# Layer norm from running sums, masks for two heads at a time, and another order for the first feed-forward products

## The chip, the core and the metric

The kernel runs on one core of one Trainium2 chip. A core has five engines that run side by side, each through its own list of instructions in order: TensorE (PE in the profile; its weight loads are PEld) multiplies matrices into PSUM, VectorE (DVE) and ScalarE (ACT) work on rows of up to 128 partitions, GpSimd (POOL) does small things, and SyncE (SP) issues transfers. They wait for each other by semaphores. The metric is the device time of one execution in microseconds. Before the change it is 3044.09 us, the median of three runs (3042.1 to 3045.04).

## What is computed

64 graphs of 256 nodes with 256 features go through two layers. All is float32.

```python
# layer 0, per graph
h = gat(gat(x, adj, W1, a1), adj, W2, a2)      # softmax over masked, leaky sums of two vectors, times rows
h = ln(x + h)
h = ln(h + relu(h @ w_ff1 + b) @ w_ff2 + b)    # 256 -> 1024 -> 256
# layer 1, per graph: 8 heads of 32, values chosen by adj
attn = softmax(q @ k.T / sqrt(32))
out = sum over r of (attn * (adj == r)) @ v_r
x = ln(h + out @ Wo + bo)
x = ln(x + gelu(x @ W1 + b1) @ W2 + b2)
```

`ln` subtracts the mean of a row of 256, divides by the root of its variance plus 1e-5, multiplies by g and adds beta. It is done four times for each graph.

## The kernel before

Two graphs make a pair, and a pair takes the whole way: the two graph layers (`gat_layers`, L528 to L557), a feed-forward (stage 0), the attention, a feed-forward (stage 2). Rows lie as 128 partitions by 256 features, four such blocks a pair. The first feed-forward product (L681) needs the rows transposed; each feed-forward does it with seven products of quarter blocks instead of eight (class `Blocks`, steps p1 to p7 for two slabs a and b). Between these stand copies on ScalarE (L687), additions on VectorE (L392) and activations (L693): product 6 can start when the copy of product 1 is there, 7 after the copy of 6, 4 after that of 7. The second product (L712) sums over the 1024 hidden columns.

The order of all instructions is written by a planner, not by hand. Python generators, one for each pair, yield the steps of TensorE with the events and PSUM banks they need; `put` hands a piece of work to one of the other engines with an estimated duration, a rank and events. `run` (L213) keeps a clock for each engine, takes whichever engine can go on first, and emits its next piece; each engine then runs its pieces in that order. Four pairs are under way at a time, besides a short generator at the start. Only one pair may be in the graph layers, one in the attention and one in a feed-forward of either stage (`alone`). Of the steps that could go, TensorE takes those outside a feed-forward first, then those of the oldest pair; so feed-forwards fill the gaps of the rest.

Around the change:
- `add_rows` (L570) adds a product from PSUM to the rows of a graph. `layernorm` then takes statistics on VectorE (L582 to L585), the power -0.5 on GpSimd (L588, L589), the normalising on ScalarE (L593), g and beta on VectorE (L598).
- `transposed` turns 32 by 32 blocks on VectorE (L618), stores to memory (L623) and gathers from it with four transfers (L629); SP issues them.
- In the graph layers a row of 1024 numbers is stored (L478) and spread to all partitions (L482) before VectorE weighs with it (L499, L501) and ScalarE scales by the inverse of the sums (L509).
- In the attention a quarter is one graph and four heads. `scores` makes its products (L796, arrays of 32 rows), ScalarE the exponentials (L803), VectorE the masked copy (L807) and the sum of two halves (L811); `products` multiplies with the values (L825) and sums columns (L828, arrays of 32 columns). VectorE inverts the sums (L837), multiplies (L838), and ScalarE reads the largest values for a check of ranges (L835). `into_rows` (L847) applies Wo.

Tiles for these are handed out in turn from pools: eight of a, m and h each with one head.

A second kernel for inputs outside the ranges is in the program too; it is not run here.

## Time and profile before

| | us |
|---|---|
| median of three runs | 3044.09 |
| profiled execution, first to last instruction | 3047.2 |
| TensorE busy | 2996.3 |
| VectorE busy | 2556.8 |
| ScalarE busy | 1752.5 |
| GpSimd busy | 252.6 |

The profiled execution has its own time, 3.1 us above the median. Its page gives the busy time of each engine, then groups of instructions by line with their number, their busy time, the mean duration of one and the idle time of the engine before them. In the waits, "A <- B: 9.1, 18, 1.4" says that A waited 9.1 us in total for B, 18 times, at most 1.4. In the timeline a line has the start and the length in us, engine, line, operation, out<-in and the number of instructions merged; in brackets stands the idle time before and what ended it. A float32 product shows as two records. The granted clock of TensorE was 0.995 over the span.

### The profile page before, as it was taken

The page shows a single profiled execution, that of the slowest core. Times are in us where ns is not written, and L with a number is a line of the kernel's source. Part 1 is how long each engine was busy: PE and PEld are TensorE (multiplying, and loading weights), DVE is VectorE, ACT ScalarE, POOL GpSimd, SP SyncE. Part 2 cuts the span into 40 slices and gives each one's busy share as a digit, 9 for nine tenths or more (in the row PEclk, how much of TensorE's full clock was granted, in tenths as well). Part 3 has the DMA queues.
Part 4 walks back from the last instruction along what each step waited for, and adds up shares of the span by engine and source line. Part 5 has one row for each costly group of instructions (what it writes and reads, how often), then busy time and mean ns, then how long its engine had stood idle before and what let it go on. Part 6 is the DMA issues. An engine that isn't in the chain of part 4 may idle for free.

```text
span 3047.2 us, 52870 instructions
## 1 busy us (share of the span) xinstructions
PE 2996.3 (98%) x19146; PEld 2452.5 (80%) x19146; DVE 2556.8 (84%) x5993; ACT 1752.5 (58%) x4096; POOL 252.6 (8%) x518
## 2 busy tenths in 40 slices
PE   7999999999999999999999999999999999999998
PEld 6887788878888888888888888888888888788876
DVE  5888988788988888888889888889888898888875
ACT  4556666556556556555565565565555655555654
POOL 0100010001100001100001000011000011000100
PEclk8999999999999999999999999999999999999999
DMA  5211041212212222112222112221122221122100
GB/s 186 74 47 61 32 127 54 70 56 84 70 40 66 77 84 77 53 53 70 84 84 77 39 60 77 84 77 62 50 68 79 84 77 52 52 71 70 49 1 22
DMA packets 211147, 205.76 MB, mean 68 GB/s; under 512 B 22336, under 2 KB 170432, under 8 KB 210880
## 3 DMA queue, kind: packets, MB, share of 16 engines
q1 hardware_dynamic: 210464, 202.06, 20.6%
q8 instruction: 153, 2.51, 0.4%
q14 instruction: 114, 0.93, 0.1%
q10 hardware_dynamic: 416, 0.26, 0.0%
HBM read 137.51 MB, written 64.73 MB: 66 GB/s over the span
## 4 chain that ended last, share of the span: by engine, by line
PE 63%; DVE 25%; DMA 6%; ACT 2%; SPq 1%; issue 1%; POOL 0%; DVEq 0%; ACTq 0%; POOLq 0%
PE ps L712 21%; PE ps L681 15%; PE ps L825 5%; DVE x L598 4%; PE ps L759 4%; PE ps L754 4%; PE ps L544 3%; DVE h L837 3%; PE ps L796 3%; DMA home<-yb 3%; DVE st L582 2%; DVE m L807 2%; PE ps L557 2%; DMA rows<-row 2%; DVE ff L392 2%; PE ps L847 2%
## 5 line engine op out<-in xcount | busy, mean ns | idle before, releaser
L712 PE MATMUL ps<-w_L_gnn_w_ff,ff 128*128 128x256 f32 x2048 | 470.9, 381 | 0.0
L712 PE MATMUL ps<-w_L_gnn_W,ff 128*128 128x256 f32 x2048 | 456.1, 380 | 1.8 <-ACT ff L693 1.8
L593 ACT ACTIVATE x<-x,less,rstd 128x256 f32<-128x256 f32 x512 | 279.2, 596 | 294.8 <-POOL less L589 294.7
L712 PEld LDWEIGHTS ps<-w_L_gnn_w_ff,ff 128*128 128x128 f32 x2048 | 386.6, 190 | 61.5 <-issue 9.8
L712 PEld LDWEIGHTS ps<-w_L_gnn_W,ff 128*128 128x128 f32 x2048 | 388.2, 190 | 57.6 <-ACT ff L693 2.6
L588 POOL TENSOR_TENSOR rstd<-rstd,mhalf 128x2 f32<-128x2 f32 x256 | 198.3, 775 | 2765.7 <-DVE less L585 2638.0
L807 DVE TENSOR_TENSOR m<-a,adj 128x512 f32<-128x512 f32 x512 | 350.1, 684 | 57.9 <-ACT a L803 57.8
L803 ACT ACTIVATE a<-ps 128x512 f32<-128x512 f32 x512 | 268.0, 604 | 222.6 <-PE ps L796 222.5
L681 PE MATMUL ps<-yT,w_L_gnn_W1p 128*128 128x256 f32 x1280 | 315.2, 382 | 4.7 <-ACT ff L687 2.4
L392 DVE TENSOR_TENSOR ff<-ps,ff 128x512 f32<-128x512 f32 x384 | 262.7, 685 | 66.4 <-PE ps L681 58.3
L681 PE MATMUL ps<-yT,w_L_gnn_w_ff1p 128*128 128x256 f32 x1280 | 308.8, 382 | 6.8 <-ACT ff L687 5.9
L681 PEld LDWEIGHTS ps<-yT,w_L_gnn_w_ff1p 128*128 128x128 f32 x1280 | 240.6, 190 | 50.8 <-ACT ff L687 18.8
L687 ACT ACTIVATE ff<-ps 128x512 f32<-128x512 f32 x384 | 223.9, 590 | 98.4 <-PE ps L681 97.6
L681 PEld LDWEIGHTS ps<-yT,w_L_gnn_W1p 128*128 128x128 f32 x1280 | 240.2, 190 | 48.2 <-ACT ps L835 8.5
L837 DVE RECIPROCAL h<-ps 128x256 f32<-128x256 f32 x128 | 223.4, 1746 | 21.3 <-PE ps L828 20.9
L509 ACT ACTIVATE xw<-xw,rs 128x258 f32<-128x258 f32 (+1 forms) x256 | 115.9, 502 | 200.7 <-DVE rs L504 200.6
L693 ACT ACTIVATE ff<-ff,c_L_gnn_b_ff 128x256 f32<-128x256 f32 x384 | 171.6, 504 | 97.4 <-DVE ff L392 97.0
L693 ACT ACTIVATE ff<-ff,c_L_gnn_b 128x256 f32<-128x256 f32 x384 | 173.3, 501 | 85.0 <-DVE ff L392 83.8
L811 DVE TENSOR_TENSOR h<-a 128x256 f32<-128x256 f32 x512 | 213.9, 418 | 0.0
L582 DVE BATCH_NORM_STATS2 st<-x 128x6 f32<-128x256 f32 x512 | 206.0, 402 | 0.9
L570 DVE TENSOR_TENSOR x<-ps,x 128x512 f32<-128x512 f32 x256 | 170.2, 682 | 16.4 <-PE ps L712 9.3
L769 ACT ACTIVATE qk<-ps,bqk 128x256 f32<-128x256 f32 x256 | 106.6, 468 | 112.2 <-PE ps L754 111.9
(128 smaller groups left out, 5008.1 us busy)
## 6 DMA issues: line engine op xcount, KB each, us to landing
home<-yb SPq DMA_DIRECT2D x182, 256.0 KB, 2.0
yT<-home SPq DMA_DIRECT2D x728, 64.0 KB, 2.0
rows<-row SPq DMA_DIRECT2D x60, 512.0 KB, 4.0
input<-in_xT SPq DMA_DIRECT2D x32, 512.0 KB, 5.1
x<-in_x SPq DMA_DIRECT2D x32, 512.0 KB, 3.8
out<-x SPq DMA_DIRECT2D x32, 512.0 KB, 5.1
input<-in_adjT SPq DMA_DIRECT2D x30, 512.0 KB, 4.5
v<-in_adjT SPq DMA_DIRECT2D x2, 512.0 KB, 7.3
```

The lines of the kernel that those rows point to most:

```text
L392: nc.vector.tensor_tensor(self.target(c, h), self.bank[bank], self.target(c, h), ALU.add)
L582: nc.vector.bn_stats(st[:, j, :], rows[j])
L588: nc.gpsimd.tensor_tensor(rstd, rstd, mhalf[:, :2], ALU.pow)
L593: nc.scalar.activation(rows[j], rows[j], AF.Identity, bias=less[:, j:j + 1], scale=rstd[:, j:j + 1])
L681: nc.tensor.matmul(to, lhsT=w1[:, a, (t + slab) * P:(t + slab + 1) * P], rhs=b, **flags)
L687: return put("scalar", 0.5, lambda: nc.scalar.activation(target(c, h), blocks.bank["x"], AF.Copy), event, rank=-1)
L693: evacuated[h][m] = put("scalar", 0.4, lambda m=m, to=to, source=source: nc.scalar.activation(to, source, func, bias=b1[:, m:m + 1]), even ...
L712: nc.tensor.matmul(p2[:, j * D:(j + 1) * D], lhsT=f[m][:, (2 * j + b) * P:(2 * j + b + 1) * P], rhs=w2[:, m, :], start=m == 0, stop=m == N ...
L803: nc.scalar.activation(a[n][o], ps[o], AF.Exp)
L807: nc.vector.tensor_tensor(m[n][o], a[n][o], adj, ALU.mult)
L811: nc.vector.tensor_tensor(h[n][o], a[n][o][:, :N], a[n][o][:, N:], ALU.add)
L837: there = put("vector", 1.68, lambda: nc.vector.reciprocal(s, po[:, N:]), there, rank=0)
```

## The change

- Layer norm: the row addition is done row block by row block with a running sum, which times -1/256 is minus the mean (`less`). ScalarE takes the squares of the centred rows with a running sum into a tile that nobody reads (`unread`). VectorE centres and multiplies by g in one operation, GpSimd makes the power -0.5, VectorE multiplies by it and adds beta in one operation. In a feed-forward both graphs' layer norms are planned after its last product.
- Masks and halves are made for two heads at a time; a, m and h are four tiles of two heads.
- The inverse of the sums: VectorE transposes 32 by 32 blocks, copies out eight columns, inverts these and transposes back. The check reads the eight columns.
- `products` are planned for each quarter alone, with the later scores between them, instead of two quarters together.
- `put_each` plans what was one piece with two parts as two pieces.
- TensorE's choice: first feed-forward products come first, the graph layers and attention next, second products last. The number of pairs under way rises by two steps of one at the start; one of them goes when the generator at the start has ended, so that five pairs are under way.
- Planned durations and ranks follow, and the tiles of the feed-forward are cut by quarters of the result (`f[c][h]`). A form of the second product with seven products (`by_seven`) is added, but `SEVEN` is empty, so it is never called.

Lines that only rename or set planned durations, and `by_seven` with its helpers (`means`, `last_weights`, `last_sums`), are left out:

```diff
+SEVEN = ()
...
+    unread = const.tile([P, N], F32, name="unread")
...
+        piece["first"] = behind.piece["first"] if behind else piece
+        piece["event"].piece = piece
...
+    def put_each(engine, us, emits, *events, rank=1, frees=(), needs=None, function=None):
+        before = None
+        for emit in emits[:-1]:
+            before = put(engine, us, emit, *events, rank=rank, lag=0.0, needs=needs, function=function, behind=before)
+            events, needs = [before], None
+        return put(engine, us, emits[-1], *events, rank=rank, frees=frees, function=function, behind=before)
...
         going, ways = [[besides, *next(besides)]], iter(ways)
+        together += 1
+        def degree(g):
+            if g[0] in filling:
+                return 2
+            return 0 if "ff" in (g[2] or ()) or alone.get("ff") is g[0] else 1
         together += 1
...
-                g = going[min(sure, key=lambda n: (going[n][0] is besides, "ff" in (going[n][2] or ()) or alone.get("ff") is going[n][0], n))
+                g = going[min(sure, key=lambda n: (going[n][0] is besides, degree(going[n]), n))
...
-                piece = waiting[engine].pop(min(able, key=lambda n: (waiting[engine][n]["rank"], waiting[engine][n]["ready"])))
+                piece = waiting[engine].pop(min(able, key=lambda n: (waiting[engine][n]["rank"], waiting[engine][n]["first"]["ready"])))
...
-        rows = y[:, of_graph(b), :].rearrange("p k d -> p (k d)")
-        return put("vector", 0.6, lambda: nc.vector.tensor_tensor(rows, p, rows, ALU.add), *events, frees=["bank"])
-    def layernorm(r, gb, b, *events):
+        of = {}
+        def add(j):
+            if j == 0:
+                of["less"] = small.tile([P, 2], F32, name="less", bufs=8)
+            row = y[:, 2 * b + j, :]
+            nc.vector.scalar_tensor_tensor(row, p[:, j * D:(j + 1) * D], 1.0, row, op0=ALU.mult, op1=ALU.add,
+                                           accum_out=of["less"][:, j:j + 1])
+            if j == 1:
+                nc.vector.tensor_scalar(of["less"], of["less"], -1.0 / D, None, ALU.mult)
+        return of, put_each("vector", 0.44, [lambda j=j: add(j) for j in range(2)], *events, frees=["bank"])
...
+    def layernorm(r, gb, b, added, *events):
         g, beta, _ = gb
-        st = mv = rstd = less = None
+        of, there = added
+        squares = rstd = None
         rows = [r[:, 2 * b + j, :] for j in range(2)]
-        def statistics():
-            nonlocal st, mv, rstd, less
-            st, mv = small.tile([P, 2, 6], F32, name="st"), small.tile([P, 2, 2], F32, name="mv")
-            rstd, less = small.tile([P, 2], F32, name="rstd"), small.tile([P, 2], F32, name="less")
-            for j in range(2):
-                nc.vector.bn_stats(st[:, j, :], rows[j])
-                nc.vector.bn_aggr(mv[:, j, :], st[:, j, :])
-            nc.vector.tensor_scalar(rstd, mv[:, :, 1], EPS, None, ALU.add)
-            nc.vector.tensor_scalar(less, mv[:, :, 0], -1.0, None, ALU.mult)
+        def square(j):
+            nonlocal squares
+            if j == 0:
+                squares = small.tile([P, 2], F32, name="squares", bufs=8)
+            nc.scalar.activation(unread, rows[j], AF.Square, bias=of["less"][:, j:j + 1], accum_out=squares[:, j:j + 1])
         def root():
+            nonlocal rstd
+            rstd = small.tile([P, 2], F32, name="rstd", bufs=8)
+            nc.gpsimd.tensor_scalar(rstd, squares, 1.0 / D, EPS, ALU.mult, ALU.add)
             nc.gpsimd.tensor_tensor(rstd, rstd, mhalf[:, :2], ALU.pow)
-            nc.gpsimd.tensor_tensor(less, less, rstd, ALU.mult)
-        def normalise():
-            for j in range(2):
-                nc.scalar.activation(rows[j], rows[j], AF.Identity, bias=less[:, j:j + 1], scale=rstd[:, j:j + 1])
-        def scale():
-            both = r[:, of_graph(b), :]
-            for v, op in ((g, ALU.mult), (beta, ALU.add)):
-                nc.vector.tensor_tensor(both, both, v.rearrange("p (k d) -> p k d", k=1).to_broadcast([P, 2, D]), op)
-        there = put("vector", 1.22, statistics, *events)
-        there = put("gpsimd", 1.2, root, there)
-        return put("vector", 1.2, scale, put("scalar", 0.8, normalise, there))
+        def centre(j):
+            nc.vector.scalar_tensor_tensor(rows[j], rows[j], of["less"][:, j:j + 1], g, op0=ALU.add, op1=ALU.mult)
+        def scale(j):
+            nc.vector.scalar_tensor_tensor(rows[j], rows[j], rstd[:, j:j + 1], beta, op0=ALU.mult, op1=ALU.add)
+        there = put_each("scalar", 0.54, [lambda j=j: square(j) for j in range(2)], there, rank=0)
+        centred = put_each("vector", 0.34, [lambda j=j: centre(j) for j in range(2)], there)
+        there = put("gpsimd", 1.2, root, there, rank=0)
+        return put_each("vector", 0.34, [lambda j=j: scale(j) for j in range(2)], there, centred, *events)
...
+        yield from (by_seven if stage in SEVEN else by_eight)(y, normal, f, evacuated, w2, w2_there, b)
+        for g in range(2):
+            normal[g] = layernorm(y, gb, g, normal["added"][g], *([biased[1]] if onwards else []))
+            if onwards:
+                transposed(y, normal[g], normal, g, pair, 1)
+        filling.clear()
+        done_with("ff")
+    def by_eight(y, normal, f, evacuated, w2, w2_there, last):
+        half, order, normal["added"] = NF // 2, (0, 1, 4, 5, 2, 3, 6, 7), []
+        filling.append(alone["ff"])
...
-            normal[b] = layernorm(y, gb, b, add_rows(y, p2, b, there), *([biased[1]] if onwards else []))
+            normal["added"].append(add_rows(y, p2, g, there))
...
-            there = took(1.08)
-            adj = all_adj[:, of_graph(b), :].rearrange("p k n -> p (k n)")
-            def weight(o):
-                a[n][o] = work.tile([P, 512], F32, name="a", bufs=2 * HQ)
-                nc.scalar.activation(a[n][o], ps[o], AF.Exp)
-            def mask(o):
-                m[n][o] = work.tile([P, 512], F32, name="m", bufs=2 * HQ)
-                nc.vector.tensor_tensor(m[n][o], a[n][o], adj, ALU.mult)
-            def halves(o):
-                h[n][o] = work.tile([P, N], F32, name="h", bufs=2 * HQ)
-                nc.vector.tensor_tensor(h[n][o], a[n][o][:, :N], a[n][o][:, N:], ALU.add)
-            there = [put("scalar", 0.48, lambda o=o: weight(o), there, rank=0, function="exp", needs="a", frees=["bank"])
-                     for o in range(HQ)]
-            masked.append([put("vector", 0.61, lambda o=o: mask(o), there[o], rank=0, needs="m") for o in range(HQ)] +
-                          [put("vector", 0.34, lambda o=o: halves(o), there[o], rank=0, needs="h") for o in range(HQ)])
+            there = took(1.13)
+            adj = all_adj[:, of_graph(b), :].rearrange("p k n -> p (k n)").rearrange(
+                "p (q n) -> p q n", q=1).to_broadcast([P, 2, 512])
+            def weight(q, k):
+                if k == 0:
+                    a[n][q] = work.tile([P, 2, 512], F32, name="a", bufs=HQ)
+                nc.scalar.activation(a[n][q][:, k], ps[2 * q + k], AF.Exp)
+            def mask(q):
+                m[n][q] = work.tile([P, 2, 512], F32, name="m", bufs=HQ)
+                nc.vector.tensor_tensor(m[n][q], a[n][q], adj, ALU.mult)
+            def halves(q):
+                h[n][q] = work.tile([P, 2, N], F32, name="h", bufs=HQ)
+                nc.vector.tensor_tensor(h[n][q], a[n][q][:, :, :N], a[n][q][:, :, N:], ALU.add)
+            there = [put_each("scalar", 0.48, [lambda q=q, k=k: weight(q, k) for k in range(2)], there, rank=0, function="exp",
+                              needs="a", frees=["bank"] * 2) for q in range(HQ // 2)]
+            masked.append([put("vector", 1.14, lambda q=q: mask(q), there[q], rank=0, needs="m") for q in range(HQ // 2)] +
+                          [put("vector", 0.61, lambda q=q: halves(q), there[q], rank=0, needs="h") for q in range(HQ // 2)])
...
-            there = took(2.2)
-            frees_at(there.time, ["a", "m"] * HQ + ["h"] * (HQ - 1))
-            s, to = h[n][0], qk[:, 0, c, b * N:(b + 1) * N]
+                nc.tensor.matmul(po[o * DH:(o + 1) * DH, N:], lhsT=ones, rhs=h[n][o // 2][:, o % 2], start=True, stop=True)
+            there = took(2.34)
+            frees_at(there.time, ["a", "m"] * (HQ // 2) + ["h"] * (HQ // 2 - 1))
+            s, to = h[n][0][:, 0], qk[:, 0, c, b * N:(b + 1) * N]
+            blocks = s.rearrange("p (g i) -> p g i", i=32)
+            both = []
+            def invert():
+                both.append(small.tile([P, 2, N // 32], F32, name="inverse", bufs=4))
+                nc.vector.transpose(s, po[:, N:])
+                nc.vector.tensor_copy(both[0][:, 1], blocks[:, :, 0])
+                nc.vector.reciprocal(both[0][:, 0], both[0][:, 1])
+                nc.vector.transpose(blocks, both[0][:, 0].rearrange("p (g i) -> p g i", i=1).to_broadcast([P, N // 32, 32]))
             def check():
-                for of, c in ((s, 0), (po[:, N:], 1)):
-                    nc.scalar.activation(of, of, AF.Copy, accum_out=reach[:, pair, c, n:n + 1])
-            there = put("vector", 1.68, lambda: nc.vector.reciprocal(s, po[:, N:]), there, rank=0)
-            there = put("vector", 0.34, lambda: nc.vector.tensor_tensor(to, po[:, :N], s, ALU.mult), there, rank=0)
-            put("scalar", 1.0, check, there, frees=["bank", "h"])
-            return there
+                for of in range(2):
+                    nc.scalar.activation(both[0][:, of], both[0][:, of], AF.Copy, accum_out=reach[:, pair, of, n:n + 1])
+            there = put("vector", 1.3, invert, there, rank=0)
+            put("scalar", 0.4, check, there, rank=3)
+            return put("vector", 0.34, lambda: nc.vector.tensor_tensor(to, po[:, :N], s, ALU.mult), there, rank=0, frees=["bank", "h"])
...
-        for n in (0, 2):
-            yield [*masked[n], *masked[n + 1], ready["v", 0, n // 2], ready["v", 1, n // 2]], None, 2
-            divided += [products(n), products(n + 1)]
-            if n == 0:
-                for later in (2, 3):
-                    yield from scores(later)
+        for n in range(4):
+            yield [*masked[n], ready["v", 0, n // 2], ready["v", 1, n // 2]], None, 1
+            divided.append(products(n))
+            if n < 2:
+                yield from scores(n + 2)
...
-    nc = bacc.Bacc("TRN2", target_bir_lowering=False, num_devices=1)
+    nc = bacc.Bacc("TRN2", target_bir_lowering=False, num_devices=1, dynamic_dma_scratch_size=1024)
```

## The prediction

> **What bounds the kernel now.** I read the page's busy times first, then the waits of TensorE, then a stretch of the timeline.
>
> ```profile
> span 3047.2 us, 52870 instructions
> ...
> PE 2996.3 (98%) x19146; PEld 2452.5 (80%) x19146; DVE 2556.8 (84%) x5993; ACT 1752.5 (58%) x4096; POOL 252.6 (8%) x518
> ```
>
> TensorE is busy 98% of the span; nothing that VectorE or ScalarE saves can count beyond the 50.9 us in which it is not. Of these, windows of 76 us put 21.2 in the first (start of transfers, first pair alone), 14.7 in the last, 15.0 in between.
>
> ```profile
> PE ps L557 <- ACT xw L509: 9.3, 1, 9.3
> PE ps L681 <- ACT ff L687: 9.1, 18, 1.4
> PE ps L127 <- DMA a<-in_L_gnn_W1T: 7.5, 1, 7.5
> PE ps L544 <- ACT xw L509: 4.5, 2, 3.5
> PE ps L712 <- ACT ff L693: 1.8, 2, 0.9
> ```
>
> L557, L127 and L544 are the start (the order of TensorE up to there is the same after the change). The recurring one is L681 (first feed-forward product) waiting for a copy on ScalarE. But a matmul's record (381 ns) is longer than the step to the next (x56 in 12.1 us, 216 ns a record), so up to 0.16 us of each gap hides in "busy". Counting starts that come over 0.13 us later than 216 ns allow, after the first 76 us, I find 44 stalls with 20.9 us; about half fall once per pair at the place below.
>
> ```profile
> 2598.16 0.48 DVE L499 SCALAR_TENSOR_TENSOR e<-rows,ratio 128x256 f32<-128x256 f32 x1 [2.02 <-DMA rows<-row]
> ...
> 2599.70 0.68 DVE L392 TENSOR_TENSOR ff<-ps,ff 128x512 f32<-128x512 f32 x1
> ...
> 2600.41 0.91 ACT L693 ACTIVATE ff<-ff,c_L_gnn_b_ff 128x256 f32<-128x256 f32 x2 [1.78 <-DVE ff L392]
> ...
> 2601.23 0.57 ACT L687 ACTIVATE ff<-ps 128x512 f32<-128x512 f32 x1
> ...
> 2601.86 1.13 PE L681 MATMUL ps<-yT,w_L_gnn_w_ff1p 128*128 128x256 f32 x4 [0.64 <-ACT ff L687]
> ```
>
> The cause is a transfer: VectorE stands 2.02 us before rows (L499), the feed-forward add L392 queues behind it, L693 and L687 behind that on ScalarE, and TensorE loses 0.64. In the steady part the layer-0 rows come late because SP issues four gathers of yT between row and rows (+1.67 us).
>
> A second hidden cost is the change of array shape:
>
> ```profile
> 1500.71 1.89 PE L712 MATMUL ps<-w_L_gnn_w_ff,ff 128*128 128x256 f32 x8
> 1502.53 1.15 PE L796 MATMUL ps<-qk 32*128 32x256 f32 x16
> 1503.60 1.13 PE L754 MATMUL ps<-yTa,wqk 128*128 128x256 f32 x4
> 1504.57 1.89 PE L759 MATMUL ps<-wv,yTa 128*128 128x256 f32 x8
> 1506.30 1.89 PE L712 MATMUL ps<-w_L_gnn_w_ff,ff 128*128 128x256 f32 x8
> ```
>
> Eight records take 1.73 (1504.57 to 1506.30); before L796 they take 1.82, so entering costs 0.09. The four after it take 0.97 instead of 0.87: 0.10. The last record in the other shape steps 0.304 instead of 0.196: 0.11. A visit to another shape costs 0.30 us.
>
> **What the skill says.** "TensorEngine Tiling (Array Packing)", Key Properties: changing the tiling mode drains TensorE; the trace agrees (0.09 to 0.11 at each edge). "Perfetto Trace Analysis", Identifying the Most-Contended Engine: matmul busy time is no measure of closeness to the bound, because of pipelining; agrees (98% against 80% for weight loads, and the hidden stalls). "ScalarE activation tables: per-element evaluation and per-set limits", What a function is on this engine: with the same operands an instruction costs the same whatever the function, and another set costs a 1283 ns load; the trace's loads are 1283 ns. "ScalarE: Activation LUTs", What ACT_TABLE_LOAD costs, adds 1380 ns of drain to each; the trace doesn't show it: the next instruction starts 1.30 us after the load does, so I charge 1.28.
>
> **The change, part by part.** Matmuls are the same in kind and number (SEVEN is empty, so the seven-product form is never issued); TensorE's work is unchanged.
>
> VectorE, removed: bn_stats 206.0, bn_aggr 93.2, two small operations 84.9, g and beta 350.2, row addition 170.2, masks 350.1, halves 213.9, reciprocal 223.4: 1691.9 us. Added:
> - row additions 512 x (425, L120, the same form with a running sum, + 82 for reading the sum) = 260; less 256 x 165 (L584) = 42
> - centre and scale 1024 x 475 (L499, two inputs and a per-partition scalar) = 486; 435 if they cost L120's 425
> - masks: 418 ns at 256 and 684 at 512 elements give 1.04 ns an element, so 1216 at 1024; x256 = 311; halves 256 x 684 = 175
> - reciprocal: two transposes of 256 columns, 435 each between L474's 237 (64) and L618's 698 (512), a small copy 155 (L446) and a reciprocal of 8 columns, 203 between L504's 166 and L837's 1746; 1.23 us x128 = 157.
>
> Sum 1431: VectorE falls by 261 (210 to 310) to about 2296, 75%.
>
> ScalarE: L593 279.2 and the check 150.6 go. Squares 512 x (468, L769, a bias pointer too, + 192 for the sum, L835) = 338, at most 512 x (596 + 192) = 403; check 256 x 385 = 99; the order shows 106 table loads for 70, +46. Net +53 to +118, 60%. GpSimd swaps one small operation for another: nothing. The one tile that all squares write is ScalarE's alone, in its own order; the smaller scratch for transfers makes room and moves nothing.
>
> Neither is worth anything in the middle: the order puts at least 20 us of TensorE work (mostly 40 to 75) between a row addition's matmul and the first product that reads the result, against some 12 us for the chain (layer norm 4.5, worked out below, transpose 0.7, store 2.0, four gathers 3.7, L359 0.4, hops). Both layer norms of a feed-forward are now planned after its last product; this cover hides that too. Without it the first graph's result would come up to 6.9 us later (32 records).
>
> At the end it shows. Before: from the last addition (3035.65) to the issue of out (3041.59) 5.94 us. After: additions 1.2, squares 1.2, POOL 0.9, scale 0.9, hops 0.3 = 4.5; centre runs beside POOL. **-1.4 us.**
>
> Products of one quarter at a time: before, two quarters ran back to back in the column shape. In TensorE's order the returns to the full shape rise from 171 to 197 (26 x 0.30 = 7.8) and direct steps between row and column shape from 31 to 67 (36 x 0.11 = 4.0). **+11.8 us**, on the engine that sets the end; nothing hides it. The bounds are +9 and +14.
>
> The order: first products now come before everything, second products last, and the limit rises twice by one, so five pairs are under way instead of four. Two things follow. The four gathers (or more) stand between row and rows in 14 of 60 cases instead of 24, so the stall above goes in most pairs. From the end of the gat products rows land in 6.3 to 7.5 us where SP is free (layer 1 of before) and 11.3 to 14.5 where it isn't; what the order after leaves for that in the steady part is some 8.5 us in the tightest place and 11 to 18 elsewhere. But first products run with less between them: a copy and its reader are one product apart (1.73 us) in 200 places instead of 137, so a delay on ScalarE, which also gets a 1.2 us pair of squares and 36 more loads, strikes more often. I take the 20.9 us as halved, **-10.5**: the regular half goes, the irregular half (start, end of run, 0.2 us here and there) stays. Bounds: -18 (almost none left) and +21 (twice as many), since the trace of before does not show the new order.
>
> In the waits that are new, VectorE stands before GpSimd (scale) and behind it queue masks and feed-forward adds; centre comes first and about 1.0 us of POOL is to be covered, so I charge nothing; uncovered it is at most 256 x 1 us on VectorE, which has 750 us free.
>
> Sum: 3047.2 + 11.8 - 10.5 - 1.4 = 3047.1 in a profiled execution. The median of the runs, 3044.1, lies 3.1 below the profiled one, so 3044 in runs.
>
> **Rivals.**
> - *Stalls vanish.* VectorE at 75%, five pairs and rows in time leave TensorE some 3 us of stalls: 3047.2 + 11.8 - 18 - 1.4 - 3.1 = 3036.5. For it: slices of before with only 0.3 us of stalls. Against: start and end stalls depend on few pairs being there.
> - *Slower: first products in a tight chain wait for ScalarE.* The place is the 1.73 us between a product, its copy and the next product; 0.7 us is copy and hop, so an item of over 1 us ahead of it (a load of 1.28 with its function, or two squares) stalls TensorE. It decides from about 17 us of stalls in all: as many as before give 3054, twice as many 3075. For it: 200 places for 137. Against: before, nearly all stalls trace back to rows, not to that distance.
> - *The change does nothing there.* The order rule alone may shift waits and save none; then only 11.8 - 1.4 remains, 3054, the same side as the last.
>
> **How the numbers follow.** 0.2% is 6 us, about what a measurement of this kernel can tell from no change: below 3038 faster, over 3050 slower. Forecast (stalls about halved, 3037 to 3050) 0.39, of which 0.35 same and 0.04 faster; stalls vanish 0.28, faster; slower rival with the third 0.33, of which 0.01 same. So faster 0.32, same 0.36, slower 0.32. The range drops a tenth at each end: 3031 to 3063.
>
> **What would show it.** Right: VectorE near 2300 and TensorE's instruction count unchanged; the first weighing (L499) waiting under 25 us for rows, of 44.8 before; stalls of 8 to 13 us; last addition to out in 4.5 us. Wrong: waits of first products for ScalarE copies over 15 us in the list of TensorE's waits; VectorE over 2400 (scale and centre dearer than 475); shape visits costing less than 0.2 us where a product of one quarter stands alone.

## The result and the profile after

The changed kernel takes 3033.1 us in the median (3032.0 to 3035.2, 6 runs) where the kernel before takes 3043.7; the ratio is 0.9964, with an interval of 0.9955 to 0.9974. It is faster by 0.36%. The profiled execution went from 3047.2 to 3031.0 us, 16.2 less. The time lies in the predicted range, but the likeliest case (3044) did not come; what came is nearest to the rival in which the stalls vanish (3036.5, given 0.28). By the prediction's own mark, below 3038, the change is faster.

The page of the changed kernel, its span and its busy times:

```profile
span 3031.0 us, 53040 instructions
...
PE 2997.3 (99%) x19146; PEld 2445.2 (81%) x19146; DVE 2315.8 (76%) x5865; ACT 1792.0 (59%) x4644; POOL 290.4 (10%) x518
```

TensorE's idle time fell from 50.9 to 33.7 us, and its busy time stayed (2996.3 and 2997.3): 12.0 us of changes of shape came into it, and some 11 us of stalls that hide in it went (both from the count below). All its waits in the list of waits (in total, times, longest):

```profile
PE ps L594 <- ACT xw L546: 8.7, 1, 8.7
PE ps L130 <- DMA a<-in_L_gnn_W1T: 7.3, 1, 7.3
PE ps L581 <- ACT xw L546: 3.6, 1, 3.6
PE ps L777 <- ACT ff L744: 1.0, 4, 0.2
PE ps L502 <- ACT rise L489: 0.9, 1, 0.9
PE ps L732 <- ACT ff L738: 0.7, 2, 0.5
```

The start is much as before (8.7, 7.3 and 3.6 us for 9.3, 7.5 and 4.5). The first feed-forward product behind a copy on ScalarE (L681 and L687 before, L732 and L738 now) fell from 9.1 us in 18 waits to 0.7 in 2. A first product close behind its copy, in the steady part of the changed kernel, now looks like this (timeline: start, duration, what). It is of the second feed-forward of a pair, where the stall of 0.64 us shown of before is of the first:

```profile
1504.97 1.89 PE L732 MATMUL ps<-yT,w_L_gnn_W1p 128*128 128x256 f32 x8
...
1506.03 0.60 ACT L738 ACTIVATE ff<-ps 128x512 f32<-128x512 f32 x1 [0.48 <-PE ps L732]
...
1506.69 1.03 PE L732 MATMUL ps<-sums_yT,w_L_gnn_W1p 128*128 128x256 f32 x4
1506.85 0.08 DVE L539 DVE_READ_ACCUMULATOR e<-adj,empty,e 128x1 f32 x1
1506.85 0.69 DVE L430 TENSOR_TENSOR ff<-ps,ff 128x512 f32<-128x512 f32 x1
```

The copy ends at 1506.63 and the product starts at 1506.69, right behind the eight records before it (1504.97 and 8 x 216 ns), without a wait. In the stall shown of before 0.06 us lay between copy and product too (2601.80 to 2601.86), so here nothing is to spare: the chain is as tight as the slower rival had it, only nothing is late in it.

To say where the time went I count TensorE's stalls again, with one difference from the prediction: a start after a change of array shape is allowed its usual 304 or 309 ns and counts from there, where the prediction left such starts out. Stalls over 0.13 us after the first 76 us are then 25.8 us before (the prediction's way of counting gave 20.9) and 3.8 after. Those of 0.03 to 0.13 us fell from 5.7 to 1.8, those of the first 76 us from 21.5 to 19.6. From its first to its last record TensorE takes 3028.3 us before and 3012.5 after; less all these stalls, 2975.3 and 2987.3. So the 16.2 us are: TensorE without stalls +12.0, stalls -27.8, start and tail -0.5, which adds up to -16.3.

### The profile page after: what moved, and what is told of

The parts are those of the page before. It is cut to its first block, busy times and chain, and to the rows that moved or that the text cites. A ratio compares the mean times of both kernels' runs of the same rounds, so it can differ in the third digit from the quotient of the medians.

```text
span 3031.0 us, 53040 instructions
## 1 busy us (share of the span) xinstructions
PE 2997.3 (99%) x19146; PEld 2445.2 (81%) x19146; DVE 2315.8 (76%) x5865; ACT 1792.0 (59%) x4644; POOL 290.4 (10%) x518
## 3 DMA queue, kind: packets, MB, share of 16 engines
q1 hardware_dynamic: 210464, 202.06, 20.8%
## 4 chain that ended last, share of the span: by engine, by line
PE 72%; ACT 1%; issue 0%; DVE 0%; POOL 0%; POOLq 0%; DVEq 0%; ACTq 0%
PE ps L777 23%; PE ps L732 19%; PE ps L955 6%; PE ps L887 5%; PE ps L882 5%; PE ps L924 3%; PE ps L985 3%; PE ps L581 3%; PE ps L565 2%; PE ps L594 2%; PE ps L958 1%; ACT unread L640 0%; ACT L744 0%; ACT ff L744 0%; PE ps L704 0%; ACT ff L738 0%
## 5 line engine op out<-in xcount | busy, mean ns | idle before, releaser
L777 PE MATMUL ps<-w_L_gnn_W,ff 128*128 128x256 f32 x2048 | 474.2, 383 | 1.0 <-ACT ff L744 1.0
L645 POOL TENSOR_SCALAR rstd<-squares 128x2 f32<-128x2 f32 x256 | 87.3, 341 | 2711.1 <-ACT unread L640 2710.4
L640 ACT ACTIVATE unread<-x,less 128x256 f32<-128x256 f32 x512 | 259.1, 506 | 130.1 <-DVE less L615 100.2
L937 DVE TENSOR_TENSOR m<-a,adj 128x1024 f32<-128x1024 f32 x256 | 311.0, 1215 | 28.1 <-ACT a L933 27.6
L612 DVE SCALAR_TENSOR_TENSOR x<-ps,x 128x256 f32<-128x256 f32 x512 | 197.7, 418 | 151.0 <-PE ps L777 76.2
L732 PE MATMUL ps<-yT,w_L_gnn_W1p 128*128 128x256 f32 x1280 | 307.3, 380 | 0.6 <-ACT ff L738 0.2
L732 PE MATMUL ps<-yT,w_L_gnn_w_ff1p 128*128 128x256 f32 x1280 | 304.5, 380 | 0.0
L738 ACT ACTIVATE ff<-ps 128x512 f32<-128x512 f32 x384 | 225.5, 589 | 125.6 <-PE ps L732 122.6
L732 PEld LDWEIGHTS ps<-yT,w_L_gnn_W1p 128*128 128x128 f32 x1280 | 242.2, 190 | 37.7 <-ACT ff L738 2.6
L732 PEld LDWEIGHTS ps<-yT,w_L_gnn_w_ff1p 128*128 128x128 f32 x1280 | 242.0, 190 | 37.0 <-issue 4.6
L941 DVE TENSOR_TENSOR h<-a 128x512 f32<-128x512 f32 x256 | 175.1, 684 | 0.2
L887 PE MATMUL ps<-wv,yTa 128*128 128x256 f32 x640 | 167.6, 384 | 0.0
```

Of the source, the lines that this page charges most:

```text
L612: nc.vector.scalar_tensor_tensor(row, p[:, j * D:(j + 1) * D], 1.0, row, op0=ALU.mult, op1=ALU.add, accum_out=of["less"][:, j:j + 1])
L640: nc.scalar.activation(unread, rows[j], AF.Square, bias=of["less"][:, j:j + 1], accum_out=squares[:, j:j + 1])
L732: nc.tensor.matmul(to, lhsT=w1[:, a, (t + slab) * P:(t + slab + 1) * P], rhs=b, **flags)
L738: return put("scalar", 0.5, lambda: nc.scalar.activation(target(c, h), blocks.bank["x"], AF.Copy), event, rank=-1)
L777: nc.tensor.matmul(p2[:, j * D:(j + 1) * D], lhsT=f[c][j][:, k, g * P:(g + 1) * P], rhs=w2[:, m, :], start=m == 0, stop=m == NF - 1)
L887: nc.tensor.matmul(to, lhsT=b[:, jc * P:(jc + 1) * P], rhs=wv[:, a], **flags)
```

## The experiments

Each kernel is compared with the kernel before on the same chip, where that took 3041.8 to 3044.0 us, so a difference of 2 us between rows may be the chips'. Stalls in the table are those over 0.13 us, by stretch, the first column with all of the first 76 us; "TensorE" is the time from first to last record less all stalls over 0.03 us (over 0.13 in the first 76 us). Times are medians of runs, the other columns come from the profiled execution. A change of shape is a start in another array shape than the one before it.

| kernel | time | ratio, interval | shape changes | TensorE | stalls to 76, to 600, to 2750, to end | VectorE busy |
|---|---|---|---|---|---|---|
| before | 3043.7 | | 373 | 2975.3 | 21.5, 7.4, 13.1, 5.4 | 2556.8 |
| changed | 3033.1 | 0.9955 to 0.9974 | 461 | 2987.3 | 19.6, 1.2, 2.6, 0 | 2315.8 |
| e1 new order in before | 3051.9 | 1.0016 to 1.0034 | 394 | 2980.4 | 22.0, 17.8, 0, 9.6 | 2559.3 |
| e2 old order in changed | 3075.0 | 1.0082 to 1.0116 | 498 | 2995.9 | 20.5, 5.0, 27.6, 0 | 2320.1 |
| e3 joined quarters in changed | 3078.3 | 1.0095 to 1.0129 | 370 | 2975.8 | 20.3, 6.0, 32.8, 14.5 | 2321.2 |
| e4 single quarters in before | 3130.5 | 1.0265 to 1.0300 | 459 | 2995.2 | 21.5, 11.3, 66.1, 3.2 | 2578.6 |
| e5 more VectorE, same order | 3104.0 | 1.0184 to 1.0218 | 461 | 2988.8 | 20.8, 15.4, 44.6, 3.9 | 2506.3 |
| e6 joined, margin 0.7 | 3030.2 | 0.9942 to 0.9970 | 371 | 2975.1 | 20.2, 1.7, 0.7, 12.1 | 2314.5 |
| e7 one pair fewer | 3039.1 | 0.9977 to 0.9994 | 464 | 2987.6 | 21.0, 3.0, 5.4, 0 | 2310.5 |
| e8 old choice, five pairs | 3041.7 | 0.9985 to 1.0002 | 477 | 2990.8 | 20.0, 0.2, 4.8, 0 | 2305.7 |
| e9 more VectorE, planned for | 3055.8 | 1.0029 to 1.0060 | 461 | 2987.0 | 21.6, 4.0, 15.7, 0 | 2498.5 |
| e10 margin 0.7 alone | 3044.3 | 1.0000 to 1.0017 | 482 | 2992.4 | 19.7, 2.0, 5.0, 0.7 | 2313.6 |
| e11 e6, fewer turns on TensorE | 3025.3 | 0.9928 to 0.9955 | 364 | 2970.6 | 22.1, 2.3, 0.1, 10.3 | 2316.9 |
| e12 order and reciprocals in before | 3033.1 | 0.9950 to 0.9978 | 373 | 2975.4 | 21.0, 2.1, 0.9, 11.7 | 2514.4 |

A planner makes the order, so every edit but e5's gives a new plan (in e5 every engine's instructions stand in the changed kernel's order, but for the added ones). A row shows what that plan does; a cause is taken from it only where the profile or a second row says the same.

**Order or VectorE.** Two theories: ORDER, that the stalls went because of the new choice and the fifth pair; VECTOR, that they went because VectorE has less to do. e1 puts into the kernel before:

```diff
+        together += 1
+        def degree(g):
+            if g[0] in filling:
+                return 2
+            return 0 if "ff" in (g[2] or ()) or alone.get("ff") is g[0] else 1
...
-                g = going[min(sure, key=lambda n: (going[n][0] is besides, "ff" in (going[n][2] or ()) or alone.get("ff") is going[n][0], n))
+                g = going[min(sure, key=lambda n: (going[n][0] is besides, degree(going[n]), n))
```

with `filling` set at the second products as in the change.

> The kernel before with only the new order rule (first feed-forward products first, second products last) and the fifth pair; layer norm, masks, reciprocals and joined quarters stay as before. It makes 194 visits to another array shape and 6 direct steps (171 and 31 before), so +4.2 us by 0.30 and 0.11 us each. Theory ORDER (the stalls went because of the order and the fifth pair): stalls over 0.13 us after the first 76 us fall from 20.9 us to 8 or less, the first weighing waits under 25 us for rows, and the time is about 3044 + 4 - 14 = 3034 us. Theory VECTOR (they went because VectorE has 240 us less to do, so that nothing queues long behind a late transfer): stalls stay near 20 us and the time is about 3048 us.

It came out slower, 3051.9 us, which neither theory said. The stretches show why: from 600 to 2750 us there is not one stall over 0.13 us, with VectorE as busy as before (2559.3 us), so in the steady part ORDER is right; but 17.8 us are lost from 76 to 600 us, and 9.6 at the end. Some 11 of the 17.8 fall in one place, with two long waits. The timeline of e1 at both:

```profile
315.95 1.76 DVE L845 RECIPROCAL h<-ps 128x256 f32<-128x256 f32 x1
...
319.33 1.75 DVE L845 RECIPROCAL h<-ps 128x256 f32<-128x256 f32 x1
...
319.86 0.36 ACT L843 ACTIVATE ps<-ps 128x256 f32<-128x256 f32 x1
320.16 0.18 ACT L843 ACTIVATION_READ_ACCUMULATOR ps<-ps 128x1 f32 x1
...
320.40 4.51 PE L687 MATMUL ps<-yT,w_L_gnn_W1p 128*128 128x256 f32 x12 [2.54 <-ACT ps L843]
...
328.38 2.05 PE L687 MATMUL ps<-sums_yT,w_L_gnn_W1p 128*128 128x256 f32 x4 [3.47 <-DVE sums_yT L365]
```

First, a first product (L687) waits for a PSUM bank. The bank is held until ScalarE's check (L843) has read it, the check comes after the division, and the division comes on VectorE behind a reciprocal of 1.76 us and a layer norm's statistics. The second wait is the longer, and no bank is in it: the product waits for an addition of VectorE (L365), which stands behind masks and halves. So the place shows two candidates, the hold of the bank and a full queue of VectorE.

e2 is the opposite: the changed kernel with the old choice and one pair fewer.

```diff
-        together += 1
...
-                g = going[min(sure, key=lambda n: (going[n][0] is besides, degree(going[n]), n))
+                g = going[min(sure, key=lambda n: (going[n][0] is besides, "ff" in (going[n][2] or ()) or alone.get("ff") is going[n][0], n))
```

> The changed kernel with the old choice among pairs and one pair fewer under way; layer norm, masks, reciprocals and single quarters stay new. It makes 234 visits to another shape and 30 direct steps (197 and 67 in the changed kernel), +7 us. Theory ORDER: stalls return to 15 to 25 us and the time is about 3033 + 7 + 17 = 3057 us. Theory VECTOR: stalls stay under 8 us and the time is about 3040 us. VectorE's busy time stays near 2316 us by both.

3075.0 us, with VectorE at 2320.1: 27.6 us of stalls stand in the steady part. VECTOR falls there; ORDER's 3057 was 18 us too low. e7 and e8 undo one half each.

> The changed kernel with the limit raised once only, so one pair fewer under way; all else new. 199 visits and 66 direct steps, as many as in the changed kernel. If the fifth pair is what feeds TensorE, 15 to 40 us of stalls and 3045 to 3075 us. If the choice rule alone does it, about 3034 us.

> The changed kernel with the old choice among pairs (first products no longer ahead, second products no longer last), the fifth pair kept. 213 visits and 51 direct steps, +3 us against the changed kernel. If the choice rule is what took the stalls away, 15 us or more of stalls and 3050 us or more; if the fifth pair did it, stalls under 8 us and 3034 to 3040 us.

With one pair fewer (e7) the steady part has 5.4 us of stalls, with the old choice but five pairs (e8) 4.8, with both undone 27.6. So either half alone does most of it in these plans, which neither expectation had. Of e8's 8.6 us over the changed kernel, 3.5 are changes of shape (2990.8 less 2987.3).

**VectorE's free time.** e5 keeps every engine's order and adds a pass of VectorE to each row block:

```diff
         def centre(j):
+            nc.vector.scalar_tensor_tensor(rows[j], rows[j], 0.0, rows[j], op0=ALU.mult, op1=ALU.add)
             nc.vector.scalar_tensor_tensor(rows[j], rows[j], of["less"][:, j:j + 1], g, op0=ALU.add, op1=ALU.mult)
```

> The changed kernel with one more pass over each row block on VectorE ahead of the centring (512 passes x about 0.42 us = 215 us more, VectorE back at about 83%, as in the kernel before); the planner isn't told, so every engine's order stays that of the changed kernel. The passes multiply by zero and add the row itself, so nothing changes in value. Theory ORDER, strong form (VectorE's share of busy time does not matter once the order is good): only the tail grows, by about 0.8 us, stalls stay under 8 us, about 3035 us. Theory VECTOR (its relief is what took the stalls away): stalls back at 20 us or more, 3050 us or more. A third outcome, far above 3060 us, would mean that the planned order lives from VectorE's pieces being as short as the planner thinks, not from its share of busy time, since the kernel before runs at 84% with 3044 us.

The third outcome, 3104.0 us. Its page and the first of its waits on TensorE:

```profile
PE 3023.6 (97%) x19146; PEld 2437.7 (79%) x19146; DVE 2506.3 (81%) x6377; ACT 1784.8 (58%) x4644; POOL 273.1 (9%) x518
```

```profile
PE ps L733 <- ACT ff L739: 20.4, 35, 1.8
```

VectorE is busy for 190.5 us more and still idle for a fifth of the span, yet TensorE's stalls grow by 71.7 us, counted from 0.03 us (96.9 less 25.2). This is the slower rival's mechanism, first products waiting for ScalarE's copy in a tight chain, set off from VectorE. e9 is the same work with the planner told of it:

```diff
-        centred = put_each("vector", 0.34, [lambda j=j: centre(j) for j in range(2)], there)
+        centred = put_each("vector", 0.71, [lambda j=j: centre(j) for j in range(2)], there)
```

> The same 512 extra passes on VectorE as in the run with more VectorE work, but the planner is told of them (0.71 us a row block instead of 0.34 for the centring), so every order is planned anew. 196 visits and 69 direct steps, as in the changed kernel. If the harm of the extra passes was that the order didn't allow for them, the stalls after the first 76 us fall to less than half of the 76 us of that run, and the time to 3070 us or less. If VectorE's load as such does the harm, it stays near 3104 us.

3055.8 us; the stalls after the first 76 us fall from 76.1 (63.9 and 12.2 under 0.13 us) to 25.6 (19.7 and 5.9). So with this one new plan some two thirds of the harm (48.2 of 70.9 us) go once the planner knows of the work.

**Single or joined quarters.** e3 joins the attention products of two quarters again in the changed kernel, e4 makes them single in the kernel before.

```diff
-        for n in range(4):
-            yield [*masked[n], ready["v", 0, n // 2], ready["v", 1, n // 2]], None, 1
-            divided.append(products(n))
-            if n < 2:
-                yield from scores(n + 2)
+        for n in (0, 2):
+            yield [*masked[n], *masked[n + 1], ready["v", 0, n // 2], ready["v", 1, n // 2]], None, 2
+            divided += [products(n), products(n + 1)]
+            if n == 0:
+                for later in (2, 3):
+                    yield from scores(later)
```

> The changed kernel with the attention products of two quarters run back to back again, as before the change; everything else stays new. 169 visits and 32 direct steps instead of 197 and 67: if a visit costs 0.30 us and a direct step 0.11 us, 12.3 us less TensorE time, about 3021 us in the median of runs and stalls still under 8 us. Rival (single quarters are what keeps TensorE from waiting, since a lone product can start sooner): the stalls come back by about as much, and the time is 3030 to 3036 us.

> The kernel before with only the attention products split into single quarters: 194 visits and 71 direct steps for 171 and 31, +11.3 us by the prediction's prices. If the stalls stay at about 21 us, the time is about 3055 us. Rival (the split itself thins the stalls, whatever the order and VectorE): stalls under 12 us and the time 3040 to 3046 us.

Both expectations failed by far, and to the slow side in both directions. The largest wait in total of TensorE in e3 and in e4:

```profile
PE ps L777 <- ACT ff L744: 34.9, 17, 3.7
```

```profile
PE ps L681 <- ACT a L803: 41.7, 19, 3.7
```

In e3 second products wait for the activated rows, in e4 first products for a bank that the exponentials of the scores hold. The price of the shapes is there all the same: e3's TensorE time without stalls is 11.5 us below the changed kernel's (2975.8 against 2987.3). But one edit in one stage, with the same arithmetic, can make a plan 45 us slower by its stalls. e6 adds a margin, with quarters joined:

```diff
-SLACK = 0.3
+SLACK = 0.7
```

> The changed kernel with quarters joined again and the planner's margin SLACK at 0.7 us instead of 0.3 (a product counts as ready for TensorE only 0.7 us after its inputs are expected): 171 visits and 29 direct steps, 76 table loads instead of 106. If the 45 us by which joined quarters alone were slower came from products placed too close behind what feeds them, the stalls after the first 76 us fall under 15 us and the 12 us of shape changes show: 3015 to 3030 us, the fastest so far. If they came from joining itself (two quarters wait for the later one's masks), the time stays over 3060 us.

3030.2 us: 0.7 us of stalls are left in the steady part, where e3 had 32.8, so joining as such was not the harm. 12.1 us stand after 2750 us. The margin alone, with single quarters (e10), does not help:

> The changed kernel with the margin at 0.7 us and single quarters: 217 visits and 48 direct steps for 197 and 67, +3.9 us. If the margin as such keeps TensorE fed, stalls of 3 us or less and about 3035 us, the shape changes being all that is left. If a margin only happens to suit one plan, the stalls are well over 6 us and the time is 3040 to 3055 us.

3044.3 us, 5.0 us of stalls in the steady part and 5.1 more of TensorE's own time, with 21 changes of shape more. A margin suits one plan and not another. e11 takes e6 and leaves one of three blocks of the last pairs to be turned on TensorE:

```diff
-        return (pair, stage) in ((0, 0), (1, 0), (NPAIR - 2, 2), (NPAIR - 1, 1), (NPAIR - 1, 2))
+        return (pair, stage) in ((0, 0), (1, 0), (NPAIR - 1, 2))
```

> Quarters joined, margin 0.7 us, and of the last two pairs only the last feed-forward block still transposes on TensorE, instead of three blocks of two pairs (they go through scratch like all others). 167 visits and 30 direct steps. In the run with joined quarters and margin 7 of its 15 us of stalls stood at 2980 to 2993 us, where TensorE waits for a layer norm to transpose it and then runs at half its pace for a while. If that goes, about 3022 to 3026 us; if the transfers take its place, 3030 us as before.

3025.3 us, as expected, and the lowest of all. It is 0.9941 of the kernel before, where the changed kernel is 0.9964; the two intervals only touch (at 0.9955), while e6's (0.9942 to 0.9970) overlaps with both. The way is only partly the expected one: 4.5 us are TensorE's own work (2975.1 to 2970.6, the turns that are gone) and 1.8 are stalls (12.1 to 10.3), since a wait of 3.8 us for activated rows and one of 3.1 us for a layer norm stay.

**Which arithmetic.** The first of e1's two long waits points to the reciprocal. e12 is e1 with the change's reciprocals, and with the old layer norm, the old masks and joined quarters:

```diff
...
+                nc.vector.transpose(s, po[:, N:])
+                nc.vector.tensor_copy(both[0][:, 1], blocks[:, :, 0])
+                nc.vector.reciprocal(both[0][:, 0], both[0][:, 1])
+                nc.vector.transpose(blocks, both[0][:, 0].rearrange("p (g i) -> p g i", i=1).to_broadcast([P, N // 32, 32]))
...
-            there = put("vector", 1.68, lambda: nc.vector.reciprocal(s, po[:, N:]), there, rank=0)
```

with the check behind the transposes and the bank freed by the division.

> The kernel before with the new order rule, the fifth pair and, of the arithmetic, only the short reciprocals (the bank is freed by the division, no longer by ScalarE's check behind it). 172 visits and 29 direct steps, as before. In the run with the new order alone, 17.8 us of stalls stand at 200 to 600 us, the longest where a first product waits for a bank that the check still holds behind two reciprocals of 1.75 us. If that hold is the cause, the stalls of 76 to 600 us fall under 6 us and the time is about 3036 us, without new layer norm or masks. If the backlog of VectorE as such is the cause, 12 us or more stay there and the time is about 3045 us.

3033.1 us, as fast as the whole change. The stalls of 76 to 600 us are 2.1 instead of 17.8, with VectorE at 83%:

```profile
PE 2991.2 (99%) x19146; PEld 2458.4 (81%) x19146; DVE 2514.4 (83%) x6377; ACT 1802.2 (59%) x4156; POOL 256.9 (8%) x518
```

What is left, 11.7 us at the end, is mostly the turn of the last rows on TensorE waiting for a layer norm:

```profile
PE ps L655 <- DVE x L604: 7.1, 2, 3.7
```

This was the expectation for the hold of the bank, and e12 met it. But e12 is also another plan than e1 (373 changes of shape for 394), its shorter reciprocals take work out of VectorE's queue too (2514.4 for 2559.3 us), and they were not tried apart from the earlier release of the bank. So that the reciprocals and their bank belong to the cause is shown as far as one plan shows it; which of the two it is stays open.

## Why the prediction was right or wrong

- **The failed step** is "I take the 20.9 us as halved, **-10.5**: the regular half goes, the irregular half (start, end of run, 0.2 us here and there) stays." It went too. Stalls over 0.13 us fell from 25.8 to 3.8, where the prediction's mark was 8 to 13: from 7.4 to 1.2 up to 600 us, from 13.1 to 2.6 in the steady part, from 5.4 to 0 at the end. With the small ones and the first 76 us the term measures -27.8, outside its own bounds of -18 to +21. Part of that lay outside the prediction's count: by leaving out starts at a change of shape it missed 4.9 us of stalls before, by beginning at 0.13 us a fall of 3.9, by beginning at 76 us one of 1.9. In the steady part the new choice and the fifth pair took the stalls away (e1, e2). That the total still fell inside the predicted range is owed to the width of the range, which had a case without stalls in it, not to this step.
- **Behind it** stands a second wrong step: "Neither is worth anything in the middle", said of the savings on VectorE and ScalarE. It shows cover for one chain, the layer norm's. The reciprocals sit in another: they hold a PSUM bank for which first products queue. Under the new order the plan with short reciprocals is 18.8 us faster (e1 3051.9, e12 3033.1): 15.7 of stalls from 76 to 600 us, and 5.0 of TensorE's own time, which come of the other plan; 2.1 are lost at the end. For layer norm and masks no run contradicts the sentence: e12 has neither and takes the same time as the whole change, with the 12 us of single quarters saved and 11.7 of stalls at the end in their place.
- **The regular stall** before (rows late behind gathers, L499) fits what came, and its mark came as forecast, 17.1 us of 44.8. In e1 the same wait is 1.4 us, and its steady part has no stall over 0.13 us.

```profile
DVE e L537 <- DMA rows<-row: 17.1, 12, 3.3
```

  But the mark is no measure of stalls: the wait is 33.1 us in e7 and 25.8 in e6, which stall little, and 7.4 in e3, 10.6 in e4 and 16.8 in e5, which stall most.
- **Array shapes, +11.8**: measured +12.0 (2987.3 less 2975.3). Four kernels of 370 to 373 changes of shape lie at 2975.1 to 2975.8 (before, e3, e6, e12; e11 has fewer turns and is left out), those of 461 to 464 at 2987.0 to 2988.8 (changed, e5, e7, e9), e2 with 498 at 2995.9. e4 alone, at 459 and 2995.2, lies 8 us off this line. That is not the price of shapes: after most of its long waits TensorE runs at half the granted clock for a while (the last section tells of this), and in the column shape this count leaves the slower steps in TensorE's time. Sixteen records of e4 after a wait of 3.73 us take 1.71 us from start to start (1155.23 to 1156.94) where 0.89 is usual (986.24 to 987.13):

```profile
986.24 1.07 PE L825 MATMUL ps<-a,v 128*32 128x256 f32 x16
987.13 1.05 PE L825 MATMUL ps<-m,v 128*32 128x256 f32 x16
...
1155.23 1.94 PE L825 MATMUL ps<-a,v 128*32 128x256 f32 x16
1156.94 1.75 PE L825 MATMUL ps<-m,v 128*32 128x256 f32 x16
```

  In e4 57 steps are of this kind, 0.39 to 0.41 us for 0.20 to 0.22 and some 11 us in all, which covers the 8. The changed kernel and the kernel before have none; e3 has 15, some 3 us, so its 2975.8 is that much too high.
- **Split and end**: with single quarters the end of the run costs less. The plans with single quarters lose 0 to 3.9 us after 2750 us (changed, e2, e4, e5, e7 to e10), those with joined ones, but for the kernel before with 5.4, 9.6 to 14.5 (e1, e3, e6, e11, e12). Next to the plans with joined quarters and the new order that is about what the single quarters cost; next to the kernel before it is less than half. The prediction had no such term. That finer steps fill the end better is an argument, not shown.
- **VectorE, -261**: it was -241.0, to 2315.8, inside its bounds. ScalarE +39.5, 13.5 under the lower bound of +53 to +118; why is open. GpSimd "nothing": +37.8 us, since the new first operation (L645) takes 341 ns on average where the one that went (L589) took 209; hidden, but for the tail.
- **Tail, -1.4**: from the last addition to the issue of out 4.62 us for 5.94, -1.3, as worked out:

```profile
3019.74 0.42 DVE L612 SCALAR_TENSOR_TENSOR x<-ps,x 128x256 f32<-128x256 f32 x1 [2.31 <-PE ps L777]
...
3021.47 1.12 DVE L649 SCALAR_TENSOR_TENSOR x<-x,less,b_L_gnn_g 128x256 f32<-128x256 f32 x2 [0.71 <-ACT unread L640]
3022.16 0.48 POOL L645 TENSOR_SCALAR rstd<-squares 128x2 f32<-128x2 f32 x1 [5.65 <-ACT unread L640]
3022.72 0.69 POOL L646 TENSOR_TENSOR rstd<-rstd,mhalf 128x2 f32<-128x2 f32 x1
3023.45 0.88 DVE L652 SCALAR_TENSOR_TENSOR x<-x,rstd,b_L_gnn_beta 128x256 f32<-128x256 f32 x2 [0.86 <-POOL rstd L646]
3024.36 0.37 SPq L1092 DMA_DIRECT2D out<-x  x1
```

  From the issue to the end of the span it is 6.6 us where it was 5.6, so only 0.3 is left of it. Why the last transfer ended later is open.
- **The slower rival** named a true mechanism, and the changed kernel escapes it with nothing to spare in places (the timeline above). "VectorE, which has 750 us free" was no cover: e5 used 190.5 of them and lost 71 us.

## What to carry to other kernels

Idle time of an engine is cover for a chain only if that engine's queue is short at the moment the chain needs it, so ask for each long instruction which buffer or bank is held until it ends and what the engine that sets the end does with it next. Where a planner fixes the order, a change of durations is a change of order: look at the stalls by stretch (ramp, steady part, end) before giving an average any meaning, and tell the planner of all work: 0.37 us a row block that it did not know of cost 70.9 us here, and the same work planned for 22.7. An edit that was slower in one plan is not refuted, since joined quarters cost 45 us in one plan and, with another margin and fewer turns, are part of the kernel with the lowest time here.

## What the hardware showed that I had not expected

A long wait of TensorE can have an after-effect. Windows of e1 (stretch, its length, PE busy, PEld, DVE, ACT, POOL, then the granted clock with 1.00 for full, DMA share and GB/s), around the two waits shown above:

```profile
317.50:320.30 2.80, 0.36 (x2) 0.00 (x0) 2.62 (x9) 1.01 (x6) 0.88 (x2) 1.00 0.33 93
320.30:324.50 4.20, 4.10 (x11) 3.36 (x12) 4.20 (x10) 3.44 (x8) 0.00 (x0) 0.59 0.00 0
324.50:328.30 3.80, 0.41 (x2) 0.01 (x1) 3.80 (x9) 3.57 (x8) 0.00 (x0) 0.92 0.00 0
328.30:334.50 6.20, 6.12 (x15) 4.89 (x16) 4.23 (x12) 1.22 (x3) 0.00 (x0) 0.50 0.00 0
```

After the first wait the granted clock is 0.59 and, after the second, 0.50, and records step by 0.43 us instead of 0.22, 22 of them in this place, some 4.6 us on top of the 6.2 us of waiting. After the first 76 us such a stretch followed all fourteen waits of 3.6 us or more (e1, e3, e4, e6, e11, e12), three of the five of 3.0 to 3.1, the one of 2.6, six of the fifteen of about 2.1 (e3, e4, e7) and none under 2.0 us. So below 3.6 us the length of the wait alone does not decide; what else does is not shown. The Trainium skill, "TensorE: Matmul & The Clock Gate", What's actually happening, tells of this: half the clock after an idle window of some 3.4 us, for about as long. The pace agrees, and the stretches last 3.41 us or two to four times that; the runs show it also after waits of 2.1 and 2.6 us. So a long wait of TensorE can cost well more than its length (10.8 us for 6.2 in this place), which no step of the prediction had; neither the kernel before nor the changed one has such a wait after its start.
